# Edges of the first two graphs of layer 3 made in the PSUM pool of the layers before

## The chip, the cores and the metric

The kernel runs on one core of a Trainium2 chip. The metric is the device time of one execution in microseconds (us), less being better. An execution was also recorded by the hardware profiler: its span runs from the first to the last instruction, and all times "at 5341.7" are counted from the span's start. The engines are TensorE (PE, with PEld for its weight loads), VectorE (DVE), ScalarE (ACT), GpSimd (POOL) and SyncE (SP); each works through its own instructions in order, and ACT, POOL and SP also issue transfers (DMAs).

## What is computed

Four layers work on 16 graphs of 1024 nodes with 128 features. Layer 0 is masked attention, layer 1 takes a maximum over neighbours, layer 2 sums neighbours and runs a small two-matrix network; each adds its input and normalises the rows. The part of layer 2 that matters here:

```python
x_agg = jnp.einsum('bnf,bnm->bmf', x, adjacency)
h = (1.0 + eps) * x + x_agg
y = jnp.maximum(h @ W1 + b1, 0.0) @ W2 + b2
x = _layernorm(x + where(node_mask, y, 0))
```

Layer 3 first removes edges: row by row of the adjacency matrix, each k-th remaining neighbour is dropped, and the same entry of the column too, so that later rows see it. Then three convolutions follow with the edges that are left:

```python
adj_d = _dilate(adj, mask)
deg = jnp.clip(jnp.sum(adj, axis=-1, keepdims=True), 1.0, None)
agg = jnp.einsum('bij,bjd->bid', adj, x) / deg
out = agg @ Wr + x @ Wx + b
nrm = jnp.maximum(jnp.linalg.norm(out, axis=-1, keepdims=True), NORM_EPS)
return out / nrm * mf[..., None]
```

each with a rectifier and a normalisation over all graphs behind it, and a last matrix over all three results.

## The kernel before, in words

**Layers 0 to 2** (`layers_012`) run graph by graph in a long pipeline of slots. Inside it the order of TensorE, ScalarE, VectorE and GpSimd is written out by hand: streams (attention, tables, the rest of a graph) are advanced by the planner `advance`, with costs and due times. Beside them the removal of edges (`dilation`) runs for all graphs at once, 32 rows at a time; it writes which edges are gone to `removed` in DRAM (L569). When the slots are done, the last graph still has its layer 1 end and layer 2 to do: `last = rest(B - 1)`. Fifteen of its steps are drawn at L859 to L861, then what is left of the removal, then `right.close()` frees the buffers of removal and tables, and the loop `for _ in last` draws the rest. From L859 on nothing is ordered by hand: the framework's scheduler places each instruction on its engine by its dependences, the memory it needs and its place in the program.

The names of that last part, in order: `ph` (transposes, L395), `y` and `ln_st` (sum and statistics), `ln_mv` (ten small steps on GpSimd, L219 to L228), `X` (normalised rows, ScalarE, L270), `ptr` and `xT` (transposes and their copy, L278, L280), `parts` and `left` (a split of X in three, L408, L411), `pa` (48 matmuls with the adjacency matrix, L419), `hT` (VectorE, L422), `pp` and `z` (L286, L291), `py` (L436, L440), `y` and `ln_st` again, `X` again, and the store of X (L447).

**PSUM** [...] Pool `psumA` of the layers 0 to 2 uses them all: "wide" twice two banks, "shared" two, "subset" two, the last for `pm` (L748) and `pt` (L760) of the slots. L867 closes it, and L868 opens the pool of layer 3, in which "bank" has two banks.

**Layer 3's edges** are made by `edges(b)`, one graph at a time. `load_edges` brings the removals `gone_all` (four loads issued by GpSimd, one buffer) and the transposed adjacency matrix `near` (two buffers). For each of 16 tiles of 128 x 512, five matmuls sum the removals and their transposes into a bank (`pgone`, L902 and L904), and VectorE compares (L906):

```python
nc.vector.tensor_tensor(near[:, c, s], near[:, c, s], p, op=ALU.is_gt, saturate=False)
```

The result goes to DRAM (`kept`, L907) and stays in `near`. Sixteen matmuls with ones add up the degrees (`pdeg`, L913), ScalarE copies them to `deg` (L914), and they pass through DRAM twice to be turned around (`degree` L915, `deg_t` L917). `settle(b)` takes `there` (L922) and the reciprocal (L925) from that and stores them (L923, L926), and `load_share` broadcasts the reciprocal to all partitions (L930).

`first_edges` (L1053) opens the pool `ep`, loads the weights of layer 3 (issued by ScalarE), and makes the edges of graph 0, settles them and makes the edges of graph 1. Its instructions come after those of layer 2 in the program, at L869. The loop at L1074 then takes each graph: `m` (the edges as floats, ScalarE, L937), `high` and `low` (a split of the features, L943, L945), `pagg` (32 matmuls, L950), `u` (times share, VectorE, L953), `po` and `o` (L961 to L966), squares and `length` (L976 to L981), `r_rows`, `phid` (L992), a second `pagg`, and the edges of the graph two ahead.

Of the kernel before, what the change touches and what calls it, by code (L numbers as in the profile page):

```python
# [31 lines left out]
BF = mybir.dt.bfloat16  # L32
# [8 lines left out]
P = 128  # L41
# [30 lines left out]
def tile_graph_layers(ctx: ExitStack, tc, a, out):  # L72
# [7 lines left out]
    psum = None  # L80

    def wide(name, tag="wide", bufs=2):
        return psum.tile([P, N], F32, tag=tag, name=name, bufs=bufs)

    def bank(name, dtype=F32):
        return psum.tile([P, 2048 // (2 if dtype == BF else 4)], dtype, tag="bank", name=name, bufs=2)


    setup = ctx.enter_context(ExitStack())
    psum = setup.enter_context(tc.tile_pool(name="psum0", bufs=2, space=PSUM))  # L90
# [19 lines left out]
    def weight(name, shape=(P, P), how=None, pool=consts):  # L110
        t = pool.tile(list(shape), F32, name="w_" + name)
        src = a[name] if how is None else a[name].rearrange(how[0], **how[1])
        nc.scalar.dma_start(out=t, in_=src)
        return t

    def column(name, n=1, pool=consts):
        return weight(name, (P, n), ("(c p) -> p c", {"p": P}), pool)
# [17 lines left out]
    def in_three(v, name):  # L135

        p = bank("p3")
        nc.tensor.matmul(p[:, :P], ones[0:1, :], v, start=True, stop=True)
        left = temp.tile([3, P], F32, name="left_b")
        nc.vector.tensor_copy(left, p[:3, :P])  # L140
        e = consts.tile([3, P], BF, name=name)
        nc.vector.memset(e, 0.0)
        for i in range(3):
            part = temp.tile([3, P], BF, name="part_b")
            nc.vector.tensor_copy(part, left)
            if i < 2:
                nc.vector.tensor_sub(left, left, part)
            nc.vector.scalar_tensor_tensor(e, part, ident[:3, i:i + 1], e, op0=ALU.mult, op1=ALU.add)
        return e
# [9 lines left out]
    nc.gpsimd.dma_start(out=half_mask, in_=a["nodemask"])  # L159
    nm = consts.tile([P, T, B], F32, name="nm")  # L160
    pm = bank("pm")
    for t in range(T):
        nc.tensor.transpose(pm[:, t * B:(t + 1) * B], half_mask[:, t * P:(t + 1) * P], ident[:B, :B])
# [30 lines left out]
    def transposed(dst, src):  # L194

        for h in range(2):
            p = bank("ptr")
            for t in range(4):
                nc.tensor.transpose(p[:, t * P:(t + 1) * P], src[:, 4 * h + t, :], ident)
            nc.scalar.copy(dst[:, halves[h]], p)  # L200
# [33 lines left out]
                mybir.DependencyClass.NoSync, mybir.DependencyReason.SCHED_ONLY), reason="pace")  # L234

    def layers_012():
        nonlocal psum
        right = es.enter_context(ExitStack())
        psums = es.enter_context(ExitStack())
        psum = psums.enter_context(tc.tile_pool(name="psumA", bufs=1, space=PSUM))  # L240
# [623 lines left out]
        right.close()  # L864
        for _ in last:
            pass
        psums.close()  # L867
        psum = ctx.enter_context(tc.tile_pool(name="psum", bufs=2, space=PSUM))  # L868
        first_edges()  # L869

# [23 lines left out]
    def edges(b):  # L896

        gone, near = load_edges(b)
        for c in range(T):
            for h, s in enumerate(halves):  # L900
                p = bank("pgone")
                nc.tensor.matmul(p, ident_b, gone[:, c, s], start=True, stop=False)  # L902
                for t in range(4):
                    nc.tensor.matmul(p[:, t * P:(t + 1) * P], gone[:, 4 * h + t, c * P:(c + 1) * P], ident_b,  # L904
                                     start=False, stop=(t == 3))
                nc.vector.tensor_tensor(near[:, c, s], near[:, c, s], p, op=ALU.is_gt, saturate=False)  # L906
        nc.sync.dma_start(out=kept[b], in_=near)  # L907

        deg = ep.tile([1, N], F32, name="deg")
        for s in halves:  # L910
            p = bank("pdeg")
            for c in range(T):
                nc.tensor.matmul(p, ones_b, near[:, c, s], start=(c == 0), stop=(c == T - 1))  # L913
            nc.scalar.copy(deg[:, s], p[0:1, :])  # L914
        nc.sync.dma_start(out=degree[b], in_=deg)  # L915
        d = ep.tile([T, P], F32, name="deg_t", bufs=2)
        nc.sync.dma_start(out=d, in_=degree[b].rearrange("(t i) -> t i", t=T))  # L917
        return near, d

    def settle(b, d):  # L920
        z = ep.tile([T, P], BF, name="there_t")
        nc.vector.tensor_scalar_min(z, d, 1.0)  # L922
        nc.sync.dma_start(out=there[b].rearrange("(t i) -> t i", t=T), in_=z)  # L923
        nc.vector.tensor_scalar_max(d, d, 1.0)
        nc.vector.reciprocal(d, d)  # L925
        nc.sync.dma_start(out=share[b].rearrange("(t i) -> t i", t=T), in_=d)  # L926
# [126 lines left out]
    def first_edges():  # L1053
        nonlocal ep, Wr, Wx, bs, gs, bes, Wl, bl
        ep = ctx.enter_context(tc.tile_pool(name="ep", bufs=1, side="right"))
        Wr, Wx, bs, gs, bes = ([f(f"L3_gnn_{w}{l}", pool=ep) for l in (1, 2, 3)] for w, f in (
            ("Wr", weight), ("Wx", weight), ("b", column), ("g", column), ("be", column)))
        Wl = weight("L3_gnn_Wl", (P, 3, P), ("(c p) o -> p c o", {"p": P}), ep)
        bl = column("L3_gnn_bl", pool=ep)
        ahead[0] = edges(0)  # L1060
        settle(0, ahead[0][1])
        ahead[1] = edges(1)

    with ExitStack() as es:
        layers_012()
# [104 lines left out]
```

## Time and profile before

| what | us |
|---|---|
| three runs: median, least, most | 6616.69, 6604.93, 6620.51 |
| the profiled execution, its own time | 6613.2 |
| its span | 6611.5 |
| slots of layers 0 to 2, to the start of layer 2's end (span start to 5290) | 5290 |
| seam from there to layer 3's first o | 104 |
| the first loop of layer 3 over the graphs (5394 to 6052) | 658 |
| the rest of layer 3 (6052 to the end) | 559 |

Over the whole span TensorE is busy 86%, VectorE 80%, ScalarE 56% and GpSimd 58%; the granted TensorE clock is 0.90 of full speed on average. Such shares say little about a seam of 104 us: there TensorE is busy 68.7 us, VectorE 33.6, ScalarE 28.3 and GpSimd 16.5, the granted clock is 0.78, and the DMA engines are busy for half of the time. The rows shown below have the start, the duration and the instruction with its line; in brackets stands how long the engine was idle before it, and what ended that.

### The profile page before, as it was taken

What the parts mean: (1) busy time and instruction counts of PE and PEld (TensorE: products, weight loads), DVE (VectorE), ACT (ScalarE), POOL (GpSimd) and SP (SyncE); (2) the same over time, 40 slices, a digit from 0 to 9 for tenths busy, and PEclk for the clock granted to TensorE, in tenths of its full rate; (3) what the DMA queues carried; (4) which work ended last, traced back from release to release, by engine and by line L of the source; (5) the groups of instructions that cost most, each with busy time, mean ns of one, the idle gap of its engine ahead of it and who ended that gap; (6) DMA issues with size and microseconds to landing.
All of it is one profiled execution on the core that took longest, in us unless ns stands there. A gap on an engine that the chain in (4) does not pass through costs nothing. (4 is left out here: it accounts for less than half of the span.)

```text
span 6611.5 us, 85916 instructions
## 1 busy us (share of the span) xinstructions
PE 5697.7 (86%) x27306; PEld 2883.8 (44%) x27306; DVE 5317.7 (80%) x8130; ACT 3733.9 (56%) x6537; POOL 3844.7 (58%) x11285
## 2 busy tenths in 40 slices
PE   6989898989898989899888898888888768787986
PEld 3434344444444444444444444444443345555643
DVE  3989899999999999999999999999998834444453
ACT  4656566666666666666666656666655523333841
POOL 2675767676767776766666676767676511110126
PEclk8989898989898989898989899999987779888997
DMA  5121212121212121212112212121110156563635
GB/s 37 14 27 22 30 24 36 20 27 26 28 28 27 27 27 26 28 26 31 28 29 30 27 26 27 26 27 28 25 25 9 32 93 120 105 124 102 230 128 166
DMA packets 478381, 317.02 MB, mean 48 GB/s; under 512 B 301162, under 2 KB 429668, under 8 KB 473828
## 3 DMA queue, kind: packets, MB, share of 16 engines
q0 software_dynamic: 105648, 84.20, 14.6%
q1 hardware_dynamic: 367600, 226.13, 11.7%
q8 instruction: 214, 3.51, 0.2%
q10 hardware_dynamic: 4676, 1.19, 0.1%
q14 instruction: 243, 1.99, 0.1%
HBM read 412.71 MB, written 117.18 MB: 80 GB/s over the span
## 5 line engine op out<-in xcount | busy, mean ns | idle before, releaser
L831 DVE TENSOR_TENSOR best<-best,pg 128x1024 f32<-128x1024 f32 x2720 | 3234.4, 1210 | 309.0 <-PE pg L779 300.5
L749 ACT ACTIVATE hot<-pm,one_less 128x512 fp32r<-128x512 f32 x2752 | 1882.3, 688 | 1115.1 <-PE pm L748 1102.9
L779 PE MATMUL pg<-hot,high 64*128 64x512 f32 x5504 | 1479.1, 534 | 453.6 <-DVE best L831 417.8
L779 PE MATMUL pg<-hot,low 64*128 64x512 f32 x5504 | 1173.3, 423 | 0.0
L748 PE MATMUL pm<-AT,lit 120*128 120x512 fp8e4 x2752 | 1143.8, 416 | 9.3 <-ACT hot L749 6.2
L779 PEld LDWEIGHTS pg<-hot,high 64*128 64x128 f32 x5504 | 547.9, 196 | 1265.1 <-DVE best L831 792.4
L616 POOL TENSOR_SCALAR sc<-low_counts,half_mask,rest 16x1 f32<-16x1 f32 x992 | 435.7, 439 | 399.6 <-DVE rest L603 305.8
L779 PEld LDWEIGHTS pg<-hot,low 64*128 64x128 f32 x5504 | 573.4, 205 | 0.0
L748 PEld LDWEIGHTS <-lit 120*128 120x128 fp8e4 x2752 | 274.5, 100 | 624.8 <-issue 560.8
L621 POOL TENSOR_SCALAR sc<-sc 16x1 f32<-16x1 f32 x992 | 430.1, 434 | 105.0
L770 ACT CAST low<-pt 128x256 fp32r<-128x256 f32 x688 | 255.6, 371 | 396.3 <-PE pt L768 392.1
L980 POOL TENSOR_TENSOR length<-length,mhalf 128x8 f32<-128x8 f32 x48 | 78.9, 1644 | 571.7 <-DVE length L979 571.7
L618 POOL TENSOR_SCALAR sc<-sc 16x1 f32<-16x1 f32 x992 | 341.8, 345 | 107.7
L624 POOL TENSOR_SCALAR last_rank<-V,sc 16x31 f32<-16x31 bf16 (+30 forms) x992 | 387.1, 390 | 0.0
L623 POOL TENSOR_SCALAR hit<-V,sc 16x31 bf16<-16x31 bf16 (+30 forms) x992 | 372.5, 376 | 0.0
L768 PE MATMUL pt<-high,less 128*128 128x256 f32 x688 | 303.2, 441 | 66.3 <-ACT high L763 58.9
L467 DVE TENSOR_TENSOR sub<-sub,q 128x24 f32<-128x24 f32 (+11 forms) x768 | 306.6, 400 | 24.6 <-ACT q L289 10.5
L619 POOL TENSOR_SCALAR sc<-sc 16x1 f32<-16x1 f32 x992 | 270.1, 272 | 83.3
L937 ACT CAST m<-near 128x1024 fp32r<-128x1024 fp8e4 x256 | 253.3, 1044 | 112.7 <-DVE near L906 59.8
L760 PE MATMUL pt<-ident,sub 128*128 128x128 f32 x1376 | 293.9, 298 | 24.7 <-ACT hot L749 22.0
L377 PE MATMUL pav<-v,eT 128*128 128x128 f32 x2048 | 307.6, 296 | 2.1 <-ACT eT L370 2.1
L617 POOL TENSOR_SCALAR sc<-sc 16x1 f32<-16x1 f32 x992 | 256.6, 259 | 86.6
(258 smaller groups left out, 9495.7 us busy)
## 6 DMA issues: line engine op xcount, KB each, us to landing
removed<-gone SPq DMA_DIRECT2D x128, 256.0 KB
An<-in_adj_dram POOLq DMA_DIRECT2D x16, 1024.0 KB, 15.1
E<-in_adj_dram POOLq DMA_DIRECT2D x128, 128.0 KB, 6.8
gone_all<-removed POOLq DMA_DIRECT2D x64, 256.0 KB, 12.1
near<-in_adjT_dram POOLq DMA_DIRECT2D x16, 1024.0 KB, 17.3
h<-x SPq DMA_DIRECT2D x32, 512.0 KB
kept<-near SPq DMA_DIRECT2D x16, 1024.0 KB
share<-share SPq DMA_DIRECT2D x32, 512.0 KB
```

What stands on the lines that cost most here:

```text
L377: nc.tensor.matmul(pav, eT[:, c, :], values[b][:, c, :], start=(c == 0), stop=(c == T - 1))
L467: nc.vector.tensor_max(sub[:, :n_g, n:2 * n], sub[:, :n_g, 0:n], qg[:, 2 * g0:2 * g0 + n_g, k:k + 1].to_broadcast([P, n_g, n]))
L616: gp.tensor_scalar(half, mine, half_mask[:, m], rest[:, n:n + 1], op0=ALU.mult, op1=ALU.add)
L618: gp.tensor_scalar(sf, half, 5.5, sf, op0=ALU.is_gt, op1=ALU.mult)
L621: gp.tensor_scalar(to, at, sf, none, op0=ALU.subtract, op1=ALU.subtract)
L623: gp.tensor_scalar(hit[:, n, n + 1:], V[:, n, n + 1:], at, None, op0=ALU.is_equal)
L624: gp.tensor_scalar(last[:, n + 1:], V[:, n, n + 1:], to, None, op0=ALU.is_le)
L748: nc.tensor.matmul(pm, lit[:, r, :], AT[b * (T + 1) + c][:, halves[h]], start=True, stop=True)
L749: nc.scalar.activation(hots[s][:, halves[h]], pm, AF.Relu, bias=one_less)
L768: nc.tensor.matmul(pt, less, high, start=False, stop=True, skip_group_check=True)
L779: nc.tensor.matmul(pg[:, a], part[rows, at * P:(at + 1) * P], hots[s][rows, halves[h]], start=(k == 0), stop=(k == 1))
L831: nc.vector.tensor_max(own, own, pg)
```

## The change

The call of `first_edges()` moves up, from behind the opening of layer 3's PSUM pool to before the closing of the old one. While it runs, the helper `bank` takes its tiles by the tag "subset" of the old pool instead of "bank"; a variable holds the tag, and is set back afterwards. The instructions themselves, their number and their operands stay; in the program they still come after those of `last`.

```diff
+    bank_tag = "bank"
+
     def bank(name, dtype=F32):
-        return psum.tile([P, 2048 // (2 if dtype == BF else 4)], dtype, tag="bank", name=name, bufs=2)
+        return psum.tile([P, 2048 // (2 if dtype == BF else 4)], dtype, tag=bank_tag, name=name, bufs=2)
...
     def layers_012():
-        nonlocal psum
+        nonlocal psum, bank_tag
...
         right.close()
         for _ in last:
             pass
+        bank_tag = "subset"
+        first_edges()
+        bank_tag = "bank"
         psums.close()
         psum = ctx.enter_context(tc.tile_pool(name="psum", bufs=2, space=PSUM))
-        first_edges()
```

## The prediction

> Lines are those of the kernel before; the changed kernel's later ones stand two or four lower. Times are us from the start of the profiled span.
>
> **What bounds the kernel now.** The change touches one seam, where the last graph's layer 2 ends and layer 3 begins, so I read first the chain of waits from 5260 to 5430 (start, duration, what; I leave pieces out):
>
> ```profile
> 5311.74 11.47 PE pa L419 x44
> ...
> 5348.07 3.63 PE pdeg L913 x16
> 5351.72 0.58 ACT deg L914
> 5352.32 5.16 DMA degree<-deg
> 5357.50 4.55 DMA deg_t<-degree
> ...
> 5363.54 4.66 DMA share<-deg_t
> 5368.21 6.57 DMA share<-share
> 5374.81 1.22 DVE u L953
> ...
> 5385.85 3.62 PE pdeg L913 x16
> ...
> 5394.34 1.12 ACT o L966
> ```
>
> From the end of layer 2 (X, written until 5341.7) to layer 3's first useful step (o, 5394.34) there are 52.7 us, and the chain in it is the edges of graphs 0 and 1: half of the tiles of graph 0, its degrees, four small transfers in a row (22.5 us from 5352.3 to 5374.8), then the tiles and degrees of graph 1. The convolution of graph 0 (pagg) ended at 5359.1 and was waiting for the last transfer. From 5394 on, the kernel repeats a pattern of some 45.7 us a graph (the length rows L980 stand 45 to 46 us apart), and the compiled order of all engines is the same in both kernels from there on. So what the seam gains at o is carried to the end.
>
> Then the table by stretches (length, then busy time of PE, PEld, DVE, ACT, POOL, then granted clock, DMA share, GB/s):
>
> ```profile
> 5240.00:5270.00 30.00, 25.80 (x77) 10.26 (x78) 29.81 (x27) 15.51 (x24) 0.12 (x1) 0.50 0.10 36
> 5290.00:5300.00 10.00, 1.97 (x8) 1.57 (x8) 2.93 (x10) 1.20 (x2) 3.36 (x10) 0.50 1.20 113
> 5300.00:5312.00 12.00, 5.50 (x13) 1.86 (x14) 0.00 (x0) 7.13 (x13) 4.24 (x2) 0.50 0.29 28
> ```
>
> While the last graph's layer 2 waits on ScalarE and GpSimd (5294 to 5312), VectorE has nothing to do and TensorE is mostly idle. That is where the edges can go. Then the timeline, for who held whom:
>
> ```profile
> 5334.61 4.02 DVE L906 TENSOR_TENSOR near<-near,pgone 128x512 fp8e4<-128x512 fp8e4 x6
> 5341.75 0.11 DVE L1001 MEMSET extra<- 3x64 uint32 x1 [3.12 <-ACT X L270]
> 5348.24 2.42 POOL L891 DMA_DIRECT2D gone_all<-removed  x4 [9.77 <-PE pgone L904]
> 5364.48 0.58 PE L902 MATMUL pgone<-gone_all,ident_b 128*128 128x512 fp8e4 x1 [5.38 <-DMA gone_all<-removed]
> ```
>
> A tile costs VectorE 0.67 (4.02 / 6). A memset into layer 3's buffers stood in VectorE's queue and held the edges 3.12 us until X was done. The load of graph 1's removals can start only when all 16 tiles of graph 0 are read (one buffer), so it began at 5348.2.
>
> **The change, part by part.** No arithmetic is added: 32 edge tiles, two degree sums, the same loads. They take the two banks named "subset" of the old pool, free since ScalarE's last hot (5276.4); the new pool opens after them.
>
> *Graph 0's tiles move up.* In the compiled order TensorE's 16 tiles (80 matmuls) follow the transposes ph (end 5293.8): four whole tiles, four mixed with the eight transposes ptr, three before the first pair of pa, the rest before its 44; one small matmul is left behind pp. VectorE does 15 before hT. Their data are there: the group gone_all has its last landing at 5271.8 + 12.3 = 5284.1, and near of graph 0, issued at 5272.3, landed 22.1 later, 5294.4, when VectorE is still at ln_st (to 5296.0). TensorE at half clock needs some 0.85 a tile (L902 0.43, four L904 0.43). Followed through the queue, ptr 8 ends at 5305.1 instead of 5303.6, since pieces of tiles 5 to 8 stand between transposes that come every 0.40 from ScalarE: +1.6 on the path through xT, parts, left, parts. VectorE is free until hT (5318.6), and tile 15 is done by 5313. In return one near tile no longer stands between y and ln_st of the last norm: -0.7.
>
> [...] The row: the 44 pa matmuls took 11.46, the first eight 0.43 each, the later ones 0.217, because they started at clock 0.50. [...] pa costs 44 x 0.217 = 9.5: -2.0. Against it stands the first row of the table: TensorE was busy 25.8 of 30 us and the clock stayed at 0.50[...]. [...] Then GpSimd: the compiled order puts three of graph 1's four removal loads after left, where they wait only for the last small matmul (5323.6) with nothing behind them, and the fourth inside the last norm's chain, 0.6 each to issue: +0.6 on X. Sum for X: -0.5 to +1.5; I take 0, X ends at 5341.7 as before. In SyncE's queue kept, degree and deg_t of graph 0 come ahead of X's store, and there ahead of h. The DMA stood empty from 5324 to 5342 (share 0.00), so the megabyte of kept delays nobody; h is issued at 5346.2 instead of 5342.6.
>
> *Degrees of graph 0.* pdeg follows py (5331.7) and costs 3.5; deg is copied by 5335.8, before X on ScalarE; degree 5.16 and deg_t 4.55 land at 5345.7 instead of 5362.1. On VectorE there_t stands behind graph 1's first tile; the fourth removal load is issued at 5334.6 and takes 6.1 to 7.6 alone (the first of each group of four), so that tile is done at 5342.5 and deg_t is later. ([...] With the 14.3 of the slowest landing in the trace it lands at 5348.9, and the sum loses 4.) Then reciprocal to 5347.9, share 4.66 and its load 6.57: 5359.3, no longer what u waits for.
>
> *Graph 1's tiles, and what is exposed.* From 5345.7 VectorE does there_t, memset, deg_t, tile 18, reciprocal, then tiles 19 to 32 with low after tile 28: 15 tiles at 0.69 (the first few at TensorE's cold 0.85), 1.25 for low, 1.8 for the small ones: the last tile ends at 5359.5. TensorE's order now has pagg of graph 0 behind all that, because its banks belong to the new pool: pdeg ends 2.5 after the last tile (as before, 5386.6 to 5389.1), 5362.0; ptr 1.5; pagg, hidden before, 7.4 to 5370.9; from there to o 4.35, as the steady pattern has it (5665.2 to 5669.6, u of 1.22 included): 5375.2. m and high need X at 5341.7 and 8 x 1.05 + 1.05: 5351.2, or 5352 if h lands late; low comes at 5355.5. Graph 2's loads are released at 5350 (near, by m) and 5358 (removals, by tile 32); with 20.7 and 14.3, the longest seen here, they are in by 5373, and its first tile is due 11.4 after o, at 5387.
>
> *Sum.* 5394.3 - 5375.2 = 19.1. Against the profiled execution's own 6613.2 (span 6611.5) this is 6594.1. That execution lies 3.5 below the median of the three runs (6616.69; 6604.9 to 6620.5) and 0.6 below the mean of all four, so I forecast **6595**. A measurement of this kernel can tell about 0.3%, 20 us, from no change; 6596.8 is that bound.
>
> **The rivals.**
> *Given back at pagg.* pagg now waits for the last edge of graph 1. If the fourth removal load lands at 5348.9 (4), TensorE stays cold through tiles 19 to 32 (0.17 x 14 = 2.4) and layer 2 pays its 1.5, the gain is 11: 6603. For it: the clock row above. Against: before, tiles from 5342.5 and from 5376.7 reached full rate within 3.7 us.
> *Slower: layer 2 held behind the edges.* Matmuls run in order, and ptr now stands behind tiles that need near of graph 0. If that load is late, all of layer 2 waits, at one for one. It landed at 5294.4 with 1.6 to spare; the price is its delay less that, and it eats the whole gain from a landing at about 5315 on, 43 us after issue; a landing at 5335 costs 20 more than before, 6634. For it: two such loads, the removals and the weights share a busy DMA (1.20 in the table), and the second near took 32.0 (landing times of near's two loads, least, median, most):
>
> ```profile
> DMA to landing us min/median/max: 22.1/27.1/32.0
> ```
>
> Against it: their issue is not moved, so nothing makes it later.
> *No effect,* if the scheduler had left the tiles where they were. The compiled order excludes it; only waits could restore it, as in the first rival.
> *More.* A warm array in all of layer 2 and in graph 1's tiles gives 19.1 + 0.5 + 2 = 21.6, with a favourable set of runs 6587.
>
> **How the numbers follow.** Forecast 0.71, given back 0.18, slower 0.06, more 0.05. Own range of the forecast 6588 to 6602 (the mechanism by 4 either way, the runs' own spread by 5). To hold 8 in 10 it takes the first rival with the spread of runs at the upper end and the last at the lower: 6584 to 6607. Faster by over 0.3%: 0.52 of the forecast's 0.71 (its centre lies just past the bound), and the last rival: 0.57. Slower 0.06. Within: 0.37, the rest of the forecast and what is given back.
>
> **What would show it.** Near tiles on VectorE from 5296 with hT not later than 5320; pdeg of graph 0 before X; degree issued near 5336; u released by pagg, not by share; o of graph 0 about 19 earlier, and the length rows 45 to 46 apart as before. ptr waiting for VectorE, X ending after 5344, or pagg starting after 5368 would prove it wrong.

## The result

| | before | changed |
|---|---|---|
| median of seven runs (us) | 6614.4 | 6591.8 |
| least, most | 6594.9, 6620.5 | 6576.7, 6593.8 |
| span of the profiled execution | 6611.5 | 6590.1 |

The ratio is 0.9963, with a 95% interval of 0.9950 to 0.9977: faster by 0.37%. The forecast was 6595 with a range of 6584 to 6607.

The times of whole executions are a poor measure of a change of 20 us here. In the 14 profiles of this study ScalarE's last `p`, the last step of the slots (L389 before, L391 changed), starts anywhere between 5275.9 and 5303.1, and the work of the slots is the same in all of them. So from here on I use the *seam*: from the start of that `p` to the start of layer 3's first `o`. Before it took 103.6 us (5290.75 to 5394.34, one profile), changed 79.3 (5289.15 to 5368.45), and in two more profiles of the changed kernel 79.6 and 79.7. The gain in the seam is 24.3, where 19.1 was forecast; the three profiles of the changed kernel agree within half a microsecond.

The chain of waits of the changed kernel from 5280 to 5375 (start, duration, what). It answers to the first fence of the prediction:

```profile
5310.94 9.67 PE pa L421 x44
...
5332.15 5.47 DMA gone_all<-removed
...
5340.46 0.86 DVE deg_t L929
...
5351.52 3.61 PE pdeg L917 x16
5355.13 0.71 issue
5355.84 1.06 PE ptr L201 x8
5356.90 7.31 PE pagg L954 x32
5364.30 1.24 DVE u L957
...
5368.45 1.12 ACT o L970
```

The four small transfers in a row are gone from the chain. In their place stands one load, `gone_all`, and from the end of `pdeg` the convolution `pagg` is on the path with its full 7.31. It was hidden before, behind the broadcast of share.

The table by stretches of the changed kernel (length, busy time of PE, PEld, DVE, ACT, POOL, then clock, DMA share, GB/s):

```profile
5240.00:5270.00 30.00, 26.19 (x79) 10.10 (x76) 29.34 (x27) 15.25 (x23) 1.19 (x2) 0.50 0.10 36
5290.00:5300.00 10.00, 7.46 (x37) 5.19 (x38) 5.95 (x15) 1.95 (x6) 3.36 (x10) 0.50 1.19 117
5300.00:5312.00 12.00, 9.18 (x69) 5.61 (x68) 6.87 (x11) 5.65 (x9) 4.25 (x2) 0.93 0.15 14
```

The idle time of before is filled: from 5300 to 5312 VectorE goes from 0.00 to 6.87 and TensorE from 5.50 to 9.18, and the clock from 0.50 to 0.93. And the timeline of the changed kernel:

```profile
5294.29 1.27 DVE L910 TENSOR_TENSOR near<-near,pgone 128x512 fp8e4<-128x512 fp8e4 x2
...
5315.97 0.75 DVE L424 SCALAR_TENSOR_TENSOR hT<-xT,eps,pa 128x512 f32<-128x512 f32 x1 [6.16 <-PE pa L421]
...
5333.24 0.29 SPq L919 DMA_DIRECT2D degree<-deg  x1
5336.72 0.28 SPq L921 DMA_DIRECT2D deg_t<-degree  x1
5338.80 0.69 DVE L910 TENSOR_TENSOR near<-near,pgone 128x512 fp8e4<-128x512 fp8e4 x1 [7.23 <-PE pgone L908]
5339.25 0.35 SPq L449 DMA_DIRECT2D x<-X  x1
...
5339.40 0.21 DVE L926 TENSOR_SCALAR there_t<-deg_t 8x128 bf16<-8x128 f32 x1
...
5364.30 1.22 DVE L957 TENSOR_TENSOR u<-pagg,share 128x1024 f32<-128x1024 f32 x1 [12.24 <-PE pagg L954]
```

Graph 0's tiles start at 5294.3, `hT` is not held by them, `degree` goes out before X is done, `u` is released by `pagg` and no longer by a DMA. VectorE waits 7.23 for the first tile of graph 1, whose fourth removal load is the one in the chain, and `there_t` follows that tile without a wait of its own.

After the first `o` nothing more is gained; the prediction had the gain there carried to the end. From the first `o` to the last one (of 48) it takes 1039.7 before and 1041.7 changed, from there to the end of the span 177.4 and 179.9. With the 1.6 by which this changed execution came earlier to the seam, 1.6 + 24.3 - 2.0 - 2.5 = 21.4, the difference of the spans. Whether these 4.5 come from the change is not shown. There is one profile of the kernel before; the two further ones of the changed kernel have 1042.3 and 1040.8, then 179.9 and 179.3, and the kernels of the experiments lie between 1038.2 and 1040.5, and between 177.5 and 180.2. The first stretch is longest of all in the three profiles of the changed kernel, so some of its 2.0 may be real.

### The profile page after: what moved, and what is told of

It is laid out like the page before. It is cut to its first block, busy times and chain, and to the rows that moved or that the text cites. A ratio compares the mean times of both kernels' runs of the same rounds, so it can differ in the third digit from the quotient of the medians.

```text
span 6590.1 us, 85790 instructions
## 1 busy us (share of the span) xinstructions
PE 5677.2 (86%) x27177; PEld 2881.5 (44%) x27306; DVE 5316.3 (81%) x8130; ACT 3735.9 (57%) x6537; POOL 3856.2 (59%) x11285
## 5 line engine op out<-in xcount | busy, mean ns | idle before, releaser
L750 PE MATMUL pm<-AT,lit 120*128 120x512 fp8e4 x2752 | 1137.9, 414 | 17.8 <-ACT hot L751 10.1
L469 DVE TENSOR_TENSOR sub<-sub,q 128x24 f32<-128x24 f32 (+11 forms) x768 | 306.7, 400 | 24.6 <-ACT q L291 10.5
```

Of the source, the lines that this page charges most:

```text
L469: nc.vector.tensor_max(sub[:, :n_g, n:2 * n], sub[:, :n_g, 0:n], qg[:, 2 * g0:2 * g0 + n_g, k:k + 1].to_broadcast([P, n_g, n]))
L750: nc.tensor.matmul(pm, lit[:, r, :], AT[b * (T + 1) + c][:, halves[h]], start=True, stop=True)
```

## The experiments

Four questions: what the early tiles cost layer 2, what the clock did, what graph 1's place in the PSUM costs, and why the two small transfers came out shorter than before. Each kernel is told by its seam. The kernel times named beside it are mostly of single runs on several chips, and are not set against each other.

**One. Only graph 0's edges in the old pool.**

```diff
@@ first_edges()
-        ahead[1] = edges(1)
@@ after the new pool is opened
+        ahead[1] = edges(1)
```

> Only graph 0's edges are made in the old pool; graph 1's are made in the new pool, behind its opening. I measure the seam from the start of p (layer 1's last rectifier, ScalarE) to the start of layer 3's first o: 103.6 us in the kernel before (5290.75 to 5394.34), 79.3 in the changed one (5289.15 to 5368.45). Theory (graph 0's edges alone must move; graph 1's tiles come up by themselves, because their buffer is free and the compiled order on the engines is nearly the same): seam 78 to 80, with a quarter of pagg between the last tiles. Rival (both graphs have to be in the old pool): graph 1's tiles fall behind pagg again, seam 90 or more.

Measured: the seam is 77.2, the kernel 6580.1. Graph 1's edges owe nothing to the old pool: moved back behind the new pool's opening they do as well, and 2.1 better, since some of `pagg` now runs between them (it starts 59.0 after `p` instead of 67.5). So the whole gain of the change can be had from graph 0's edges alone.

**Two. A second buffer for graph 1's removals,** so that its loads needn't wait for graph 0's tiles.

```diff
...
-        ahead[1] = edges(1)
+        with tc.tile_pool(name="spare", bufs=1, side="right") as spare:
+            ahead[1] = edges(1, spare)      # gone_all of graph 1 in its own buffer
```

> The changed kernel with a second buffer for graph 1's removals, so that their loads need not wait for graph 0's tiles. In the compiled order all 16 tiles and the degrees of graph 0 and four tiles of graph 1 then stand in TensorE's queue ahead of the transposes ptr of layer 2. Theory (matmuls in order hold layer 2 behind edges, at one for one): the first ptr some 9 us later after p than in the changed kernel (9.7 there), X ends 9 later, and though no edge is left after X, the seam is 79 to 85, no better than 79.3. Rival (the wait of 5.2 us for the fourth removal load is what is left to gain): seam 74.

Measured: seam 97.3, kernel 6610.3. Worse than either expected. The timeline of this kernel:

```profile
5323.64 1.29 DVE L910 TENSOR_TENSOR near<-near,pgone 128x512 fp8e4<-128x512 fp8e4 x2 [13.87 <-DMA near<-in_adjT_dram]
5324.38 0.59 PE L906 MATMUL pgone<-gone_all,ident_b 128*128 128x512 fp8e4 x1 [10.28 <-DVE near L910]
...
5326.05 0.42 PE L280 MATMUL ptr<-ident,X 128*128 128x128 f32 x1
```

With the buffer free, the scheduler put graph 0's remaining tiles, its `pdeg` and tiles of graph 1 ahead of layer 2's transposes `ptr` on TensorE. Graph 1's `near` had not landed, VectorE waited 13.87 for it, TensorE 10.28 for VectorE, and the first `ptr` came 32.3 after `p` instead of 9.7. This is the rival "layer 2 held behind the edges" made real. The one buffer of the changed kernel, which delays graph 1's load, also keeps its tiles out of layer 2's way.

**Three. Graph 0's near made late,** by 1 MB more ahead of it in the same queue.

```diff
@@ first_edges()
+        with tc.tile_pool(name="spare", bufs=1, side="right") as spare:
+            late = spare.tile([P, T, N], F8, name="late")
+            nc.gpsimd.dma_start(out=late, in_=adjT[1].rearrange("(c p) i -> p c i", p=P))
```

> The changed kernel with a further load of one megabyte, whose data nobody reads, issued ahead of graph 0's loads. In the queue of transfers near of graph 0 should land some 10 us later. Theory (ptr stands behind tiles that need near, and there is next to no slack): the first near tile on VectorE and ptr 7 to 9 us later after p, the seam 86 to 89. Rival (the tiles give way, or layer 2 had slack): seam 79 to 81.

Measured: seam 89.8, kernel 6601.7. From the chain of waits of this kernel:

```profile
5276.83 18.39 DMA near<-in_adjT_dram
5295.22 0.96 DVE ln_st L267 x5
5296.19 11.52 issue
...
5307.80 0.70 DVE near L910
```

The 18.39 is not the whole load: it landed 30.8 after its issue (21.6 in the changed kernel), and the 11.52 put down to "issue" are VectorE's wait for it. Counted from `p`, it landed 12.9 later than in the changed kernel. The first near tile comes 11.7 later, the first `ptr` 10.1, the end of X 10.5, and `o` 10.5. So 2.4 of the load's delay was covered (the prediction had 1.6 to spare), and the rest came out at `o`. Only this one delay was tried.

**Four. The clock alone.** The kernel before, with ten matmuls that nobody reads, five behind each of the first two `parts`.

```diff
+                if b == B - 1 and k < 2:
+                    warm = psum.tile([P, 512], F32, tag="subset", name="warm", bufs=2)
+                    for i in range(5):
+                        nc.tensor.matmul(warm, parts[:, k, i, :], An[b][:, i, :512], start=(i == 0), stop=(i == 4))
```

> The kernel before, with ten matmuls added whose result nobody reads: five behind each of the first two parts of the last graph's layer 2, where TensorE waits. Nothing else moves. Theory (the edges warm the array before pa, and that is why pa's 44 matmuls fell from 11.5 to 9.7 us): pa 44 takes 9.5 to 9.8 here too, seam 103.6 - 1.8 = 101.8. Rival (the clock stays at half, as in the slots before, and pa's shorter time came from elsewhere): pa 44 stays at 11.3 to 11.6, seam 103.6.

Measured: seam 101.4, 2.2 less than before, and in the chain of waits of this kernel:

```profile
5302.34 9.68 PE pa L423 x44
```

The 44 `pa` matmuls take 9.68 as in the changed kernel (9.67), and not 11.47 as before, with nothing else moved. In the trace of before the granted clock is 0.50 for the first 3.5 us of the 44, to 5315.2, and 1.00 from 5315.5 on; in that of the changed kernel it is 1.00 over all of them. So the shortening of `pa` is the clock's, it is a side effect of the work that now stands ahead of it, and it is worth some 2 us.

**Five. The subset's banks in a pool of their own,** which stays open, so that layer 3's pool needn't wait for graph 1's edges.

```diff
+        subset = ctx.enter_context(tc.tile_pool(name="subset", bufs=2, space=PSUM))
         psums = es.enter_context(ExitStack())
...
-        return psum.tile([P, 4, D], F32, tag="subset", name=name, bufs=2)
+        return subset.tile([P, 4, D], F32, tag="subset", name=name, bufs=2)
```

> The changed kernel with one edit: the two banks of the subset become a PSUM pool of their own that stays open through layer 3, so that the new pool doesn't have to wait for graph 1's edges before pagg of graph 0 may use its banks. Measure: from the last graph's p on ScalarE to layer 3's first o (before 103.6, changed 79.3). Theory (the banks are what puts pagg behind pdeg of graph 1, and the rest of the seam stays): pdeg of graph 1 ends at 66 after p as it did, and only the part of pagg that gets ahead of it is gained; in the compiled order TensorE still has 28 of the 32 matmuls of pagg behind pdeg, so some 1 to 2 us: 77 to 78.5. Rival (banks alone are the price, the 7.3 us of exposed pagg goes): 72 to 73.

Measured: seam 77.4, kernel 6574.8. The chain of waits of this kernel:

```profile
5343.00 3.47 PE pdeg L918 x16
5346.47 6.39 PE pagg L955 x28
```

28 of 32 matmuls of `pagg` still follow `pdeg`. The banks put `pagg` behind graph 1's edges, but with the banks free the order on TensorE keeps most of it there. 1.9 to 2.3 of the 7.3 is what the pool costs.

**Six. Graph 1's removals loaded early** (graph 0's in a buffer of its own), with graph 1's tiles kept behind graph 0's degrees.

```diff
...
-        ahead[0] = edges(0)
-        settle(0, ahead[0][1])
-        ahead[1] = edges(1)
+        with tc.tile_pool(name="spare", bufs=1, side="right") as spare:
+            ahead[0] = edges(0, load_edges(0, spare))
+            settle(0, ahead[0][1])
+            loaded = load_edges(1)              # removals behind `left` in the schedule
+            start = len(nc.cur_bb.bb.instructions)
+            ahead[1] = edges(1, loaded)
+            behind(marks["deg"], start)         # tiles behind the copy of deg of graph 0
```

Here `behind(x, start)` has the scheduler place the instructions made since `start` after x. (Not shown: `deg` of graph 0 is copied by VectorE instead of ScalarE, and one memset of layer 3 is kept from moving ahead.)

> The changed kernel with graph 0's removals in a buffer of their own, so that graph 1's four removal loads go out at once behind the last norm's start instead of three early and one 11 us later; graph 1's tiles are kept behind the copy of deg of graph 0 on every engine, so that layer 2 isn't held (as it was with the spare buffer for graph 1). Nothing of the work is changed. Theory (the wait of 5.2 us on the fourth removal load is real but mostly covered by deg_t of graph 0, which comes within 2 us of it): the seam is 76 to 77, 2 to 3 less than the changed kernel's 79.3, with pagg still exposed behind pdeg of graph 1. Rival (the fourth load is what sets the end): the tiles of graph 1 all come 5 earlier, 74. Other rival (deg_t alone decides): no change, 79.

Measured: seam 78.2, between the theory and the second rival. The fourth load is off the path, yet only 1.1 to 1.5 came of it. The chain of waits of this kernel has something else in its place:

```profile
5353.41 2.87 DMA x<-X
```

VectorE waited for X's store to be done before a small copy into one of layer 3's buffers, in the middle of graph 1's tiles, and `deg_t` stood behind that store in SyncE's queue (issued at 5353.83, 5.72 after `degree`). So this run does not tell what the load alone is worth.

**Seven. Both,** with the changed kernel beside it.

> Both edits together: the subset's banks in a pool of their own, and graph 1's removals loaded at once from the start of the last norm. Theory (after the loads are early, pagg can run beside graph 1's tiles, before pdeg of graph 1): 71 to 75 in the seam, and the kernel 5 to 8 below the changed one, 6584 to 6587. Rival (the banks of pagg don't matter, since TensorE's order keeps pagg behind the tiles): as with the early loads alone, about 77.

> The changed kernel once more, beside the version with both edits, on the same chip. Both theories: the seam 79.3 within 0.5, since it was set by the chain of graph 1's tiles, pdeg, ptr, pagg and u; the time 0.3 to 0.45% below the kernel before.

Measured: seam 74.9 with both, 79.6 changed. As times 6601.2 (ratio 0.9964, 0.9950 to 0.9977) and 6603.4 (0.9964, 0.9952 to 0.9977): five runs do not tell 5 us apart. The timeline of the kernel with both edits shows the same two waits on X:

```profile
5345.42 0.29 SPq L926 DMA_DIRECT2D degree<-deg  x1
5350.73 0.33 SPq L452 DMA_DIRECT2D x<-X  x1
5351.15 0.29 SPq L928 DMA_DIRECT2D deg_t<-degree  x1
...
5353.79 0.15 DVE L1088 COPY out_bias<-w_L_gnn_bl 128x1 f32<-128x1 f32 x1 [2.88 <-DMA x<-X]
```

`deg_t` stood behind X's store in SyncE's queue, so it was issued 5.73 after `degree`, with an empty DMA (share 0.00). And a copy of 128 numbers into one of layer 3's buffers held VectorE 2.88 in the middle of graph 1's tiles, as a memset had done for 3.12 in the kernel before.

**Eight. The DMA kept busy** while degree and deg_t of the changed kernel are under way.

```diff
...
         nc.sync.dma_start(out=degree[b], in_=deg)
+        if b == 0:
+            nc.scalar.copy(busy[0:1, 0, :8], deg[:, 512:520])
+            nc.scalar.dma_start(out=busy, in_=adjT[1, :512].rearrange("(c p) i -> p c i", p=P))
```

> The changed kernel with 2 MB loaded into a buffer that nobody reads, started from ScalarE's queue when deg of graph 0 has been copied, so that the DMA is busy while degree and deg_t of graph 0 are under way. ScalarE has about 3 us to spare there ahead of X, and SyncE's order keeps degree and deg_t ahead of X's store. Theory (the two small transfers were shorter in the changed kernel than before because the DMA was nearly empty, share 0.83 and 0.04 against 1.03 and 1.12): degree goes from 3.45 back to about 5.2 and deg_t from 2.6 to 4 to 4.5, the fourth removal load from 5.3 to 7 or more; graph 1's tiles end 3 to 4 later and the seam is 82 to 84. Rival (their length is a matter of place in the queue or of what reads them, not of the load): degree and deg_t within 0.4 of the changed kernel's, the seam 79 to 80.

Measured: seam 82.1. The chain of waits of this kernel:

```profile
5333.53 4.28 DMA degree<-deg
5337.87 4.14 DMA deg_t<-degree
```

Together 8.5, against 6.2 in the changed kernel and 9.7 before; the seam is 2.4 to 2.8 longer. Here `there_t` does wait for `deg_t`:

```profile
5342.04 0.22 DVE L930 TENSOR_SCALAR there_t<-deg_t 8x128 bf16<-8x128 f32 x1 [0.88 <-DMA deg_t<-degree]
```

The tables by stretches over these two transfers (the DMA share is the last number but one), of the kernel before,

```profile
5352.32:5357.50 5.18, 5.18 (x24) 4.26 (x23) 0.00 (x0) 0.00 (x0) 0.91 (x1) 1.00 1.03 161
5357.50:5362.05 4.55, 1.61 (x8) 0.99 (x6) 0.00 (x0) 0.00 (x0) 0.00 (x0) 1.00 1.12 124
```

of the changed kernel,

```profile
5333.24:5336.72 3.48, 0.00 (x0) 0.00 (x0) 0.00 (x0) 0.68 (x2) 2.44 (x5) 0.88 0.83 74
5336.72:5339.40 2.68, 1.65 (x10) 1.13 (x11) 0.60 (x1) 2.65 (x8) 0.00 (x0) 0.50 0.04 6
```

and of the one with the busy DMA:

```profile
5333.53:5337.87 4.34, 0.00 (x0) 0.00 (x0) 0.00 (x0) 1.74 (x5) 2.44 (x5) 1.00 0.91 83
5337.87:5342.01 4.14, 2.59 (x15) 1.71 (x16) 0.69 (x1) 1.64 (x5) 0.00 (x0) 0.54 1.03 399
```

The same 4 KB in the same place in the queue take longer with the DMA busy: `degree` 4.34 at a share of 0.91 instead of 3.48 at 0.83, `deg_t` 4.14 at 1.03 instead of 2.68 at 0.04. The theory holds in its sign and for `deg_t`; `degree` grew by only 0.9, where 1.7 was expected; the DMA share over it was 0.91, not 1.03. The fourth removal load grew too, from 5.47 to 6.85, and graph 1's first tile came 2.2 later after `p`; so the run does not split the longer seam between the load and the two small transfers. X's store and h also came 5 later in this kernel, behind share in SyncE's queue, but nothing on its chain waits for them.

**Nine. The two waits on X taken away** from the version with both edits.

```diff
-            nc.sync.dma_start(out=x3[b], in_=X[b])
+            (nc.scalar if b == B - 1 else nc.sync).dma_start(out=x3[b], in_=X[b])
...
     nc.vector.tensor_copy(pl, bl)
+    behind(marks[1, "near"], start)             # behind graph 1's last tile
...
         nc.sync.dma_start(out=x0, in_=x3[b])
+        if b == 0:
+            behind(marks[0, "deg_t"], start)
```

> The version with both edits (seam 74.9), in which two waits on X had come in: deg_t of graph 0 stood in SyncE's queue behind X's store (5.73 after degree with the DMA share at 0.00), and a small copy into one of layer 3's buffers held VectorE 2.88 in the middle of graph 1's tiles until X's store was issued. Here X's store goes out from ScalarE's queue, h is loaded behind deg_t, and the copy comes behind graph 1's tiles. Theory (both waits were on the path): tiles 9 to 16 of graph 1 start some 2 to 2.5 earlier, after which the transposes of h stand in TensorE's queue between them and hold it until h lands, so the seam is 73 to 74.3. Rival (the transposes of h decide alone): no change, 74.7 to 75.2.

Measured: seam 73.6, kernel 6579.5. The timeline and then the chain of waits of this kernel:

```profile
5330.50 0.29 SPq L927 DMA_DIRECT2D degree<-deg  x1
5331.77 0.28 SPq L929 DMA_DIRECT2D deg_t<-degree  x1
```

```profile
5335.83 4.67 DMA h<-x
...
5343.97 3.61 PE pdeg L924 x16
5347.58 7.32 PE pagg L963 x32
```

`degree` on an empty DMA (share 0.01) took 1.27, and both waits are gone. What is left is X through DRAM to `h` and its transposes, and `pagg`. It was timed with the changed kernel beside it:

> The version with both edits and without the two waits on X, once more and timed. The seam 73.6 within 0.5 (it was 73.56), that is 5.9 less than the changed kernel's 79.5, so the kernel should be 5 to 7 below the changed one, ratio to the kernel before 0.9945 to 0.996. Rival (what is gained before the first o is lost again later in layer 3, as 2 us were in the changed kernel): the same time as the changed kernel within 2.

> The changed kernel beside it on the same chip: the seam 79.5 within 0.5, ratio to the kernel before 0.996 to 0.997.

Measured: seams 74.6 and 79.7; times 6585.9 (five runs, 6577.5 to 6588.1; ratio 0.9954, 0.9940 to 0.9967) and 6581.2 (6577.5 to 6596.9; ratio 0.9955, 0.9942 to 0.9967). The seam is 5.1 shorter; that the kernel is faster is not shown. The seam missed its 73.6 by 1.0: TensorE had waited 2.6 and 2.7 for `h` in the two profiles, and in this one it came back at half rate (the five `ptr` took 1.07 instead of 0.55).

## Why the prediction was right

The direction, the mechanism and the new bound came out as argued, but for what decides graph 1's first tiles; the gain in the seam was under-estimated by 5.2. The steps of the prediction, counted from `p`:

| step | forecast | measured |
|---|---|---|
| `ptr` 8 ends later by | 1.6 | 0.8 |
| the 44 `pa` | 11.5 or 9.5; netted to "X as before" | 9.67 |
| X ends | 50.9 | 50.1 |
| deg of graph 0 copied | 45.0 | 44.1 |
| `degree`, `deg_t`, each up to what waits for it | 5.16, 4.55 | 3.48, 2.68 |
| `deg_t` is read by `there_t` | 54.9 | 50.2 |
| fourth removal load alone | 6.1 to 7.6 | 5.47 |
| last tile of graph 1 ends | 68.7 | 62.9 |
| `pdeg` of graph 1 ends | 71.2 | 66.0 |
| `ptr` of layer 3, and `pagg` exposed | 1.5, 7.4 | 1.8, 7.3 |
| first `o` | 84.4 | 79.3 |

*Graph 0's tiles move up.* Right: they fit into the idle time, `hT` came on time (5315.97 and 5320.72), and they cost layer 2 less than feared. For `pa` the forecast took a sum between 2.0 less (an estimate: all 44 at the 0.217 of the later ones) and nothing less, and what came was 1.8 less. In the changed kernel TensorE had no gap from 5298.8 to 5303, and the granted clock is 0.50 up to 5301.5 and 1.00 from 5302; experiment four shows the same shortening with nothing else changed. From the start of the work without a gap to the higher clock it took 3.0 us in this profile, 3.7 and 6.1 in two more of the changed kernel. The row that was held against the estimate comes again: at 26.19 of 30 us busy, with gaps of some 0.5 in between, the clock is 0.50 in this profile too. That row had gaps, and the work from 5298.8 to 5303 had none; that the gaps are what held the clock down was not shown.

*Degrees of graph 0.* This is the term that was mis-sized. The forecast took 5.16 and 4.55 from the trace of before. Those are the durations of two small transfers on a full DMA (share 1.03 and 1.12), and the same prediction had noted that the DMA stands empty at the place they move to. They took 3.48 and 2.68. That is 3.5 of the missing 5.2; 0.9 came with the copy of deg, that much earlier, and 1.1 from VectorE's work behind `there_t`: the small steps took 1.3 and not 1.8, and the 15 tiles 10.3, where the forecast's sum leaves them 10.8; 0.6 was lost again because `pdeg` ended 3.1 behind the last tile and not 2.5; the remaining 0.3 is made up of smaller differences. Experiment eight fills the DMA again, and the two take 2.3 of the 3.5 longer. The fourth removal load, too, was quicker than its row, 5.47 (5.2 to 5.6 in six profiles).

*What decides the first tiles of graph 1.* `deg_t` by the forecast; the fourth removal load in the trace, so this step was wrong. The load landed at 5337.62, graph 1's first tile followed at 5338.80, and `there_t`, where the 2.68 of `deg_t` end, stood behind that tile on VectorE. `deg_t` itself was there before: from 5337.95 to 5339.25 the DMA moved nothing (share 0.00), so its data were in some 1.2 after its issue at 5336.72, and the rest of the 2.68 is the wait for the tile. It cost the forecast little, since without the tile `there_t` could have come at most 1.5 sooner. What the load alone is worth stays open, because in experiment six X's store came onto the path; with the banks free the same edit gave 2.5 (77.4 to 74.9), and 3.8 once the two waits on X were gone (73.6).

*What is exposed.* Right in place and size: `u` is released by `pagg`, share is in time, and `pagg` stands behind `pdeg` with 7.31. How much of that is due to the PSUM pool was not split in the prediction. Experiments one and five put it at 1.9 to 2.5; the rest is TensorE's order.

*The rivals.* "Given back at pagg" did not come: the fourth load landed at 5337.62, and the granted clock was back at 1.00 from 5343 on, 5.3 after graph 1's first tile had begun on TensorE. "Layer 2 held behind the edges" did not come in the changed kernel, but its price, one for one beyond what is to spare, fits experiment three (10.5 lost of a delay of 12.9, so 2.4 to spare there, not 1.6), and it came in full where graph 1's loads were freed (experiment two). "More" (a seam shorter by 21.6) is nearer to the measured 24.3 than the forecast, but what was missing came mostly from the small transfers (3.5 of the 5.2), not from a higher clock. That the time of the kernel came within 4 us of the forecast is in part luck: the seam gained 5.2 more than forecast, and behind it 4.5 were not found again in the profile.

## What to carry to other kernels

A duration read from a trace carries the load of its surroundings (here `deg_t` took 4.55 at a DMA share of 1.12 and 2.68 at 0.04): when a small transfer is moved to a place where the DMA is empty, take its row from a place with that DMA share, and do the same with matmuls and the clock (the 44 `pa` took 11.47 and 9.67). A duration that ends where the reader starts can hold a wait of the reader itself (up to 1.5 of the 2.68 here). Work that is moved into idle time of an in-order engine is free only as long as its data are there (a load 12.9 later cost 10.5 at `o`), and a second buffer that lets data come earlier can let the scheduler put waiting work ahead of the path (the seam went from 79.3 to 97.3). Where whole executions differ by more than a change is worth, measure the seam it touches between two fixed events.

## What the runs showed of the hardware that was not expected

- A store of 4 KB from SBUF to DRAM, up to the next instruction in the queue that waits for it: 1.27 and 1.28 us at a DMA share of 0.01 (2 profiles), 3.3 to 3.6 at 0.80 to 0.91 with one removal load under way (6 profiles), 4.34 at 0.91 with 2 MB more queued, 4.8 to 5.2 at 1.03 to 1.06 (3 profiles). The share alone does not give the length: at 0.91 it was 3.40 in one kernel and 4.34 in another.
- A removal load of 256 KB, issued as the one before it was landing, takes 5.2 to 5.6 (6 profiles; in the changed kernel 5.47 from its issue at 5332.15, with the one before it landed at 5333.9).
- TensorE at 87% busy with gaps of about half a microsecond (0.38 to 0.56) stayed at clock 0.50 for 30 us (5240 to 5270, changed kernel). In three profiles of the changed kernel the clock went to 1.00 after 3.0, 3.7 and 6.1 us of the same work without a gap (in the last two read from the 128x512 `pgone` matmuls, 0.63 us before and 0.38 after); in the first of them it then stayed at 1.00 from 5306 to 5312 while TensorE was busy 3.4 of 6 us.
